# Cutting the minima and maxima of a quantile network so that PSUM copies stand at even distances, and taking the tiles with long lists first

## The chip, the cores and the metric

The kernel runs on one core of a Trainium2 chip. The metric is the device time of one execution in microseconds (us). A core has five engines with a queue of instructions each: TensorE (PE), VectorE (DVE), ScalarE (ACT), GpSimd (POOL) and SyncE (SP). SBUF is the working memory, 128 partitions wide; PSUM is the memory that TensorE writes its products to.

## What is computed

Two graph layers run one after the other over 4096 nodes with 128 features. Layer 0 is a graph attention layer with 8 heads. Layer 1, which the change is about, takes for each node the quartiles of its neighbours' features, feature by feature:

```python
remove = mask & ((rank + 1) % skip[:, None] == 0)
keep = mask & ~remove
n_keep = keep.sum(axis=1)
vals = jnp.where(keep[:, :, None], x[None, :, :], big)
svals = jnp.sort(vals, axis=1)
for q in (0.25, 0.5, 0.75):
    idx = jnp.maximum(jnp.ceil(q * n_keep).astype(jnp.int32) - 1, 0)
    picked = jnp.take_along_axis(svals, idx[:, None, None], axis=1)[:, 0, :]
    agg = agg + w_q * picked
agg = 0.5 * agg + 0.5 * x
out = agg @ W.T + b + x
```

About 32 of 4096 entries in a row of the adjacency matrix are set, so a node has some 32 neighbours.

## The kernel before

The first half of the execution searches the adjacency matrix for each node's neighbours and computes layer 0; the change does not touch it. The nodes are then ordered by their number of neighbours and split into 32 tiles of 128 nodes, one node to a partition, tile 0 with the shortest lists and tile 31 with the longest. `HT[t]` is half the length of the longest list of tile t after the removal; `2 * HT` slots are sorted, from 22 in tile 0 to 62 in tile 31.

A **unit** is what is sorted together: tiles 0 and 1 alone, tiles 2 to 23 in pairs, tiles 24 to 31 alone (`UNITS`, 21 of them). For each unit:

- `fetch_unit` has GpSimd issue one indirect DMA per slot and tile (`vals`, 128 rows of 128 features each, by `gather`, line 178), then one per tile for the nodes' own rows (`xs`). `vals` has two buffers, so the fetch of a unit can start once the unit two before it has read its values.
- `quantile_out` has VectorE run a selection network over the slots: in each of its rounds, minima and maxima of slots at a distance d (line 1117). `groups` joins neighbouring slots, so one instruction covers `c` runs of `m` slots, each slot 128 elements wide in a single tile and 256 in a pair. The first rounds read `vals`, the later ones two work tiles by turns, the last write the slots that can hold a quantile (`goal`).
- After every stretch of minima and maxima that a count (`ran`) puts above `BREATH` = 2.0 us, VectorE copies one element from PSUM (`still`) to `junk` (line 1126).
- ScalarE scales an identity matrix by the weight of each slot (`dg`, line 1136), TensorE sums the slots with it and applies the layer's matrix, ScalarE copies the result to `o`, and `write_out` has GpSimd scatter it to the output (line 187), one DMA per tile.

In GpSimd's queue the fetch of the next unit stands ahead of the scatters of the unit before the current one. The order of instructions on VectorE, TensorE, ScalarE and GpSimd is the order in which the program issues them. `order` sets the sequence of the units: [0], [2,3], [6,7], [10,11], [14,15], [18,19], [22,23], [25], [27], [29], [31], [30], [28], [26], [24], [20,21], [16,17], [12,13], [8,9], [4,5], [1].

Of the kernel before, what the change touches and what calls it, by code (L numbers as in the profile page):

```python
# [63 lines left out]
UNITS = [[0], [1]] + [[t, t + 1] for t in range(2, 24, 2)] + [[t] for t in range(24, NT)]  # L64
# [3 lines left out]
        HT[_t] = max((CAP[t] - 1) // 2 for t in _u)  # L68
LMAX = 2 * max(HT)
SLOTS = max(2 * HT[u[0]] * len(u) for u in UNITS)  # L70
BREATH = 2.0


R_NUM, R_OWN, R_F1 = L, L + 1, L + 2
# [22 lines left out]
def selection_network(n, targets):  # L97


    t = (n - 1).bit_length()  # L100
    stages = []
    p = 1 << (t - 1)
    while p:
        q, r, d = 1 << (t - 1), 0, p
        while True:
            stages.append((d, [i for i in range(n - d) if i & p == r]))
            if q == p:
                break
            d, q, r = q - p, q >> 1, p
        p >>= 1  # L110
    live = set(targets)
    plan = []
    for d, lows in reversed(stages):
        mins = [i for i in lows if i in live]
        maxs = [i for i in lows if i + d in live]
        plan.append((d, mins, maxs))
        for i in mins + maxs:
            live |= {i, i + d}
    return plan[::-1]


def groups(slots):

    runs = []
    for s in slots:
        if runs and s == runs[-1][0] + runs[-1][1]:
            runs[-1][1] += 1
        else:
            runs.append([s, 1])
    out = []  # L130
    i = 0
    while i < len(runs):
        b, n = runs[i]
        j = i + 1
        stride = n
        if j < len(runs) and runs[j][1] == n:
            stride = runs[j][0] - b
            while j < len(runs) and runs[j] == [b + stride * (j - i), n]:
                j += 1
        out.append((b, j - i, stride, n))  # L140
        i = j
    return out


def slots_of(tile_, g, size):

    b, k, stride, n = g
    flat = tile_[:, b * size : (b + (k - 1) * stride + n) * size]
    if k == 1:
        return flat  # L150

    return bass.AP(
        tensor=flat.tensor,
        offset=flat.offset,
        ap=[list(flat.ap[0]), [stride * size, k], [1, n * size]],
    )
# [12 lines left out]
def targets_of(unit):  # L169

    return sorted(set().union(*(quantile_slots(t) for t in unit)))
# [30 lines left out]
def kernel(  # L202
# [15 lines left out]
    nc = tc.nc  # L218
# [65 lines left out]
    parts = adjp.tile([64, N], BF16, name="parts", bufs=1)  # L284
# [155 lines left out]
    kp.release()  # L440


    order = [[t] for t in (0,)] + UNITS[2::2] + UNITS[3::2][::-1] + [UNITS[1]]
    with tc.tile_pool(name="sort", bufs=2) as sp, tc.tile_pool(name="fin", bufs=3) as fp, tc.tile_pool(
        name="fin_ps", bufs=2, space=PSUM
    ) as pp, tc.manual_schedule(engines=ORDERED):
# [2 lines left out]
        still = pp.tile([P, 1], F32, name="still", bufs=1)  # L449
        nc.vector.memset(still, 0.0)  # L450
        late = dict(ident=ident, halfid=halfid, ones=ones, WlT=WlT, bl_b=vecs[:, 3, :], still=still)
# [19 lines left out]
        for nxt in order[1:] + [None]:  # L471
            now = fetched
            if nxt:
                fetched = fetch_unit(nxt)
            if done:
                write_out(*done)
            done = quantile_out(tc, sp, fp, pp, *now, wt, late)
# [602 lines left out]
def quantile_out(tc, sp, fp, pp, unit, vals, xs, wt, late):  # L1080

    nc = tc.nc
    k = len(unit)
    n, size = 2 * HT[unit[0]], k * D
    targets = targets_of(unit)


    where = [vals] * n
    pair = [sp.tile([P, SLOTS * D], F32, name=f"work{i}", bufs=1) for i in range(2)]
    goal = sp.tile([P, TMAX * D], F32, name="goal")  # L1090
    junk = sp.tile([P, 1], F32, name="junk", bufs=1)

    def turn(v):
        return pair[1] if v is pair[0] else pair[0]

    network = selection_network(n, targets)
    final = {}
    for r, (d, mins, maxs) in enumerate(network):
        for i in mins + [i + d for i in maxs]:
            final[i] = r  # L1100
    ran = 0.0
    for r, (d, mins, maxs) in enumerate(network):
        after = list(where)
        for low, slots, op in ((0, mins, ALU.min), (d, maxs, ALU.max)):
            kinds = {}
            for i in slots:
                at = i + low in targets and final[i + low] == r
                kinds.setdefault((id(where[i]), id(where[i + d]), at), []).append(i)
            for (_, _, at), same in kinds.items():
                a, b = where[same[0]], where[same[0] + d]  # L1110
                dst = goal if at else turn(b if low else a)
                parts = groups(same)
                if at:
                    parts = [(i + q * s, 1, m, m) for i, c, s, m in parts for q in range(c)]
                for i, c, s, m in parts:
                    j = targets.index(i + low) if at else i + low
                    nc.vector.tensor_tensor(  # L1117
                        slots_of(dst, (j, c, s, m), size),
                        slots_of(a, (i, c, s, m), size),
                        slots_of(b, (i + d, c, s, m), size),  # L1120
                        op,
                    )
                    ran += 0.06 + c * m * size * 0.00104
                    if ran > BREATH:

                        nc.vector.tensor_copy(junk, late["still"])
                        ran = 0.0
                for i in same:
                    after[i + low] = dst
        where = after  # L1130

    st_ps = pp.tile([P, 2, P], F32, name="st_ps")
    for u, t in enumerate(unit):
        for j, place in enumerate(targets):
            dg = fp.tile([P, P], F32, name="dg", bufs=6)
            nc.scalar.activation(dg, late["ident"], AF.Copy, scale=wt[:, t, place : place + 1])  # L1136
            nc.tensor.matmul(  # L1137
                st_ps[:, u, :],
                lhsT=goal[:, (j * k + u) * D : (j * k + u + 1) * D],
                rhs=dg,  # L1140
                start=(j == 0),
                stop=False,
            )
        nc.tensor.matmul(
            st_ps[:, u, :], lhsT=xs[:, u, :], rhs=late["halfid"], start=False, stop=True
        )
    sT = fp.tile([P, 2, P], F32, name="sT")
    nc.scalar.copy(sT[:, 0:k, :], st_ps[:, 0:k, :])
    o_ps = pp.tile([P, 2, D], F32, name="fo_ps")
    for u in range(k):  # L1150
        nc.tensor.matmul(o_ps[:, u, :], lhsT=sT[:, u, :], rhs=late["WlT"], start=True, stop=False)
        nc.tensor.matmul(
            o_ps[:, u, :], lhsT=late["ident"], rhs=xs[:, u, :], start=False, stop=False
        )
        nc.tensor.matmul(
            o_ps[:, u, :],
            lhsT=late["ones"][0:1, :],
            rhs=late["bl_b"][0:1, :],
            start=False,
            stop=True,  # L1160
        )
    o = fp.tile([P, 2, D], F32, name="o")
    nc.scalar.copy(o[:, 0:k, :], o_ps[:, 0:k, :])  # L1163
    return unit, o
# [226 lines left out]
```

## Time and profile before

| | us |
|---|---|
| median of 3 runs | 3857.79 (3854.88 to 3884.28) |
| the profiled execution | 3857.37 |
| its span | 3855.5 |
| first gather of the quantile stage starts | 1930.2 |
| first minimum of the stage starts | 1959.35 |
| last copy from PSUM in the stage starts | 3845.3 |
| `L178 vals` gathers, 1024: mean / shortest / longest | 1.382 / 0.941 / 4.759 |
| `L1126` copies, 627: shortest / median / longest | 0.139 / 0.148 / 0.154 |
| `L187` scatters to the output, 32: mean | 2.123 |

The profile is of one execution. Its page gives the busy share of each engine in 40 equal slices of the span (one digit each, in tenths, 9 is 90% or more). Tables by stretch give the busy time and, in brackets, the number of instructions of PE matmuls, PE weight loads (PEld), DVE, ACT and POOL, then TensorE's clock, the share of the DMA engines and GB/s. In the order in time a line has the start, the duration, the engine, the source line, the operation with its output and input, and the shape; in square brackets stands how long the engine was idle before and what ended that. "A <- B: us, times" in a list of waits is the time that an engine spent waiting for B.

### The profile page before, as it was taken

What the parts mean: (1) busy time and instruction counts of PE and PEld (TensorE: products, weight loads), DVE (VectorE), ACT (ScalarE), POOL (GpSimd) and SP (SyncE); (2) the same over time, 40 slices, a digit from 0 to 9 for tenths busy, and PEclk for the clock granted to TensorE, in tenths of its full rate; (3) what the DMA queues carried; (4) which work ended last, traced back from release to release, by engine and by line L of the source; (5) the groups of instructions that cost most, each with busy time, mean ns of one, the idle gap of its engine ahead of it and who ended that gap; (6) DMA issues with size and microseconds to landing.
All of it is one profiled execution on the core that took longest, in us unless ns stands there. A gap on an engine that the chain in (4) does not pass through costs nothing. (4 is left out here: it accounts for less than half of the span.)

```text
span 3855.5 us, 21960 instructions
## 1 busy us (share of the span) xinstructions
PE 1253.7 (33%) x5433; PEld 961.2 (25%) x5433; DVE 2671.4 (69%) x6439; ACT 403.4 (10%) x603; POOL 2807.9 (73%) x2388
## 2 busy tenths in 40 slices
PE   6483867863746444455600000000000000000001
PEld 2143534543635444444500000000000000000000
DVE  8774688782522222257436888669999999998788
ACT  3111223210111101111100000000000000000000
POOL 1657674577777777777478888877788887888882
PEclk9975666655665555555555555555555555555555
DMA  6423444322222222222111111111111111111110
GB/s 213 153 88 106 150 139 132 122 54 65 54 55 53 54 53 54 64 58 55 34 47 38 41 39 34 38 42 41 41 38 28 32 35 44 38 35 38 38 40 16
DMA packets 110281, 241.25 MB, mean 63 GB/s; under 512 B 46976, under 2 KB 63360, under 8 KB 101952
## 3 DMA queue, kind: packets, MB, share of 16 engines
q0 software_dynamic: 76160, 160.24, 15.3%
q10 hardware_dynamic: 9360, 67.18, 5.1%
q1 hardware_dynamic: 24624, 12.34, 1.3%
q8 instruction: 45, 0.74, 0.1%
q14 instruction: 92, 0.75, 0.1%
HBM read 228.44 MB, written 11.15 MB: 62 GB/s over the span
## 5 line engine op out<-in xcount | busy, mean ns | idle before, releaser
L178 POOL DMA_INDIRECT vals<-x_d,idx x1024 | 1415.6, 1382 | 314.4 <-issue 303.8
L178 POOL DMA_INDIRECT G<-xt_d,idx x1180 | 1173.6, 995 | 483.4 <-issue 339.9
L1117 DVE TENSOR_TENSOR work<-work 128x256 f32<-128x256 f32 (+7 forms) x1168 | 921.5, 823 | 0.7
L1137 PE MATMUL st_ps<-dg,goal 128*128 128x128 f32 x286 | 71.9, 429 | 1791.9 <-DVE goal L1117 1704.4
L1117 DVE TENSOR_TENSOR work<-work,work 128x512 f32<-128x512 f32 (+4 forms) x820 | 584.3, 738 | 1.3
L1137 PEld LDWEIGHTS st_ps<-dg,goal 128*128 128x128 f32 x286 | 63.7, 324 | 1798.4 <-issue 1797.5
L926 PE MATMUL y<-wide,G 128*128 128x32 f32 (+3 forms) x2360 | 480.1, 382 | 21.9 <-DVE wide L914 21.9
L926 PEld LDWEIGHTS y<-wide,G 128*128 128x128 f32 x2360 | 460.0, 297 | 45.8 <-DVE wide L914 24.2
L869 DVE TENSOR_TENSOR z<-G,f1x 128x128 f32<-128x128 f32 (+2 forms) x92 | 29.9, 335 | 471.6 <-DMA G<-xt_d,idx 468.5
L1117 DVE TENSOR_TENSOR work<-vals 128x768 f32<-128x768 f32 (+11 forms) x64 | 128.8, 2028 | 267.8 <-DMA vals<-x_d,idx 265.7
L574 DVE MAX8 first<-key 128x8 f32<-128x128 f32 x1024 | 227.5, 282 | 112.5 <-PE key L610 112.5
L607 PE MATMUL key<-sgn,markb 128*128 128x512 bf16 x256 | 142.0, 555 | 160.9 <-DVE first L574 107.5
L883 PE MATMUL small<-z,own 128*4 128x32 f32 (+3 forms) x436 | 50.4, 284 | 368.1 <-ACT z L876 368.1
L1136 ACT ACTIVATE dg<-ident,wt 128x128 f32<-128x128 f32 x143 | 47.5, 394 | 1105.0 <-PE st_ps L1137 1104.6
L568 ACT ACTIVATE sgn<-adj_t 128x2048 bf16<-128x2048 int32 x64 | 122.1, 1907 | 343.0 <-PE key L607 328.2
L898 PE MATMUL rz<-rden,ownT 4*128 4x32 f32 (+3 forms) x436 | 107.1, 419 | 117.9 <-DVE rden L894 96.5
L610 PE MATMUL key<-parts,oneb 64*128 64x512 bf16 x256 | 140.6, 550 | 6.3 <-POOL parts L196 6.3
L956 PE MATMUL small<-W_sb,late 128*128 128x128 f32 x512 | 118.9, 426 | 33.6 <-DVE late L953 33.6
L898 PEld LDWEIGHTS rz<-rden,ownT 4*128 4x128 f32 x436 | 94.5, 310 | 134.0 <-DVE rden L894 68.3
L187 POOL DMA_INDIRECT out_dram<-o,own_i x32 | 67.9, 2123 | 79.9 <-ACT o L1163 56.2
L883 PEld LDWEIGHTS small<-z,own 128*4 128x4 f32 x436 | 27.1, 102 | 385.8 <-ACT z L876 373.3
L956 PEld LDWEIGHTS small<-W_sb,late 128*128 128x128 f32 x512 | 110.2, 327 | 44.9 <-DVE late L953 43.9
(179 smaller groups left out, 1879.3 us busy)
## 6 DMA issues: line engine op xcount, KB each, us to landing
adj_t<-in_adj_dram ACTq DMA_DIRECT2D x64, 1024.0 KB
G<-xt_d,idx POOLq DMA_INDIRECT x1180
vals<-x_d,idx POOLq DMA_INDIRECT x1024
R<-rec_d SPq DMA_DIRECT2D x128, 26.2 KB
xt_d<-rec SPq DMA_DIRECT2D x4, 544.0 KB
rec<-in_x_dram SPq DMA_DIRECT2D x4, 512.0 KB
W_sb<-in_L_gnn_W_dram SPq DMA_DIRECT2D x2, 512.0 KB
a_b<-in_L_gnn_a_dram SPq DMA_DIRECT2D x2, 512.0 KB
```

The lines of the kernel that those rows point to most:

```text
L178: nc.gpsimd.indirect_dma_start(out=dst, out_offset=None, in_=rows, in_offset=bass.IndirectOffsetOnAxis(ap=idx, axis=0),)
L187: return nc.gpsimd.indirect_dma_start(out=rows, out_offset=bass.IndirectOffsetOnAxis(ap=idx, axis=0), in_=src, in_offset=None,)
L568: nc.scalar.activation(sgn, adj_t, AF.Sign, accum_out=cnt[:, i : i + 1])
L574: nc.vector.max(first[:, ts(c0 // CW + c, 8)], key[:, ts(c, CW)])
L607: nc.tensor.matmul(key, lhsT=markb, rhs=sgn[:, ts(b, 512)], start=True, stop=False)
L610: nc.tensor.matmul(key, lhsT=oneb[0:64, :], rhs=parts[:, ts(r, 512)], start=False, stop=True)
L883: nc.tensor.matmul(den[0:4, :].rearrange("p (g r h) -> p r g h", r=k // 4, h=H)[:, r], lhsT=own[w][:, ts(r, 4)], rhs=z[:, layer[i] : layer ...
L898: nc.tensor.matmul(rz[:, layer[i] * H : (layer[i] + w) * H], lhsT=ownT[w][:, r, :], rhs=rden.rearrange("p (g r h) -> p r g h", r=k // 4, h ...
L926: nc.tensor.matmul(yf[:, ts(g, c)], lhsT=G[:, col + g - g0, 0:D], rhs=pf[:, ts(g, c)], start=(i == 0 and g % (w // 2) == w // 2 - 1), stop ...
L956: nc.tensor.matmul(o, lhsT=hv[:, h, :], rhs=consts["W1_sb"][:, h, :], start=(h == 0), stop=(h == H - 1))
L1117: nc.vector.tensor_tensor(slots_of(dst, (j, c, s, m), size), slots_of(a, (i, c, s, m), size), slots_of(b, (i + d, c, s, m), size), op,)
L1137: nc.tensor.matmul(st_ps[:, u, :], lhsT=goal[:, (j * k + u) * D : (j * k + u + 1) * D], rhs=dg, start=(j == 0), stop=False,)
```

## The change

The function `then` keeps a count of what VectorE has run since the last copy: 0.148 us for a first minimum or maximum, 0.071 for each further one, and 0.001042 us for each element. An instruction that would take the count over 1.7 us is cut (`cut`) to as many slots as fit in 1.45 us; if not one slot fits, a copy is issued ahead of it. A copy is issued as soon as the count is over 1.25 us.

The order of the units becomes [0], then the single tiles from [24] to [31], then the pairs from [22,23] down to [2,3], and [1].

```diff
--- before.py
+++ after.py
@@ -68,7 +68,12 @@
         HT[_t] = max((CAP[t] - 1) // 2 for t in _u)
 LMAX = 2 * max(HT)
 SLOTS = max(2 * HT[u[0]] * len(u) for u in UNITS)
-BREATH = 2.0
+TT_FIX, TT_EACH, TT_OVER = 0.148, 0.001042, 0.077
+TURN_MIN, TURN_AIM, TURN_MAX = 1.25, 1.45, 1.7
 R_NUM, R_OWN, R_F1 = L, L + 1, L + 2
@@ -140,6 +145,17 @@
         out.append((b, j - i, stride, n))
         i = j
     return out
+def cut(g, room):
+    i, c, s, m = g
+    if c == 1:
+        return [(i, 1, room, room), (i + room, 1, m - room, m - room)]
+    if m > room:
+        return [(i, 1, m, m), (i + s, c - 1, s, m)]
+    q = min(c - 1, room // m)
+    return [(i, q, s, m), (i + q * s, c - q, s, m)]
 def slots_of(tile_, g, size):
@@ -440,7 +456,9 @@
     kp.release()
-    order = [[t] for t in (0,)] + UNITS[2::2] + UNITS[3::2][::-1] + [UNITS[1]]
+    pairs = [u for u in UNITS if len(u) == 2]
+    order = UNITS[:1] + UNITS[2 + len(pairs) :] + pairs[::-1] + UNITS[1:2]
     with tc.tile_pool(name="sort", bufs=2) as sp, tc.tile_pool(name="fin", bufs=3) as fp, tc.tile_pool(
         name="fin_ps", bufs=2, space=PSUM
     ) as pp, tc.manual_schedule(engines=ORDERED):
@@ -1099,6 +1117,14 @@
         for i in mins + [i + d for i in maxs]:
             final[i] = r
     ran = 0.0
+    def then(slots):
+        return ran + TT_FIX + slots * size * TT_EACH - (TT_OVER if ran else 0.0)
+    def turn_of_gpsimd():
+        nc.vector.tensor_copy(junk, late["still"])
     for r, (d, mins, maxs) in enumerate(network):
         after = list(where)
         for low, slots, op in ((0, mins, ALU.min), (d, maxs, ALU.max)):
@@ -1112,7 +1138,19 @@
                 parts = groups(same)
                 if at:
                     parts = [(i + q * s, 1, m, m) for i, c, s, m in parts for q in range(c)]
-                for i, c, s, m in parts:
+                parts = list(parts)
+                while parts:
+                    i, c, s, m = parts.pop(0)
+                    if then(c * m) > TURN_MAX:
+                        room = int((TURN_AIM - then(0)) / (size * TT_EACH))
+                        if ran and room < 1:
+                            turn_of_gpsimd()
+                            ran = 0.0
+                            parts.insert(0, (i, c, s, m))
+                            continue
+                        if c * m > max(1, room):
+                            parts[:0] = cut((i, c, s, m), max(1, room))
+                            continue
                     j = targets.index(i + low) if at else i + low
                     nc.vector.tensor_tensor(
                         slots_of(dst, (j, c, s, m), size),
@@ -1120,10 +1158,9 @@
                         slots_of(b, (i + d, c, s, m), size),
                         op,
                     )
-                    ran += 0.06 + c * m * size * 0.00104
-                    if ran > BREATH:
-
-                        nc.vector.tensor_copy(junk, late["still"])
+                    ran = then(c * m)
+                    if ran > TURN_MIN:
+                        turn_of_gpsimd()
                         ran = 0.0
                 for i in same:
                     after[i + low] = dst
```

## The prediction

> **What bounds the kernel now.** I read the 40 slices first. From slice 21 on (1930 us, where the quantile stage begins) only VectorE (DVE) and GpSimd (POOL) have work:
>
> ```profile
> DVE   8774688782522222257436888669999999998788
> ...
> POOL 1657674577777777777478888877788887888882
> ```
>
> Neither is full throughout: DVE sits at 6 to 8 at both ends of the stage and at 9 in the middle. The table by stretch, cut at the first `work<-vals` of a unit, tells why (columns: length, then busy time and instructions of PE, PEld, DVE, ACT, POOL):
>
> ```profile
> 2327.90:2449.00 121.10, 5.93 (x28) 5.11 (x28) 87.02 (x125) 2.50 (x8) 99.13 (x69) 0.51 0.13 37
> ...
> 2888.30:3029.20 140.90, 6.04 (x23) 4.93 (x22) 140.87 (x291) 3.07 (x10) 121.81 (x63) 0.50 0.11 30
> ...
> 3423.00:3533.10 110.10, 12.12 (x56) 10.23 (x55) 92.42 (x118) 5.81 (x18) 90.94 (x63) 0.53 0.13 37
> ...
> sum 1886.35, PE 121.98 PEld 104.75 DVE 1648.58 ACT 56.59 POOL 1496.70; mean PE 8.13 PEld 6.98 DVE 109.91 ACT 3.77 POOL 99.78
> ```
>
> In a unit of two node tiles (first and third line) DVE works 87 to 92 us and then waits; in [31] (second) it never waits. Over the stage DVE works 1648.6 of 1886.3 us, and the **237.8 us** it is idle are nearly all one wait, seen from the tile it waits for:
>
> ```profile
> DVE work L1117: 233.5, 9
> POOL vals L178: 7.6, 25
> ```
>
> Nine times a sort waits for its gathers. GpSimd does not wait for buffers (7.6 us); it is slow. How slow, the order in time shows. With DVE idle a gather is issued every 1.25 us; with DVE at work:
>
> ```profile
> 2309.05 0.95 POOL L178 DMA_INDIRECT vals<-x_d,idx  x1 [0.30 <-issue]
> 2310.30 0.94 POOL L178 DMA_INDIRECT vals<-x_d,idx  x1 [0.30 <-issue]
> ```
> ```profile
> 2816.92 0.15 DVE L1126 COPY junk<-still 128x1 f32<-128x1 f32 x1
> ...
> 2816.98 0.95 POOL L178 DMA_INDIRECT vals<-x_d,idx  x1 [0.30 <-issue]
> 2816.99 1.25 DVE L1117 TENSOR_TENSOR work<-work,vals 128x1024 f32<-128x1024 f32 x1
> ...
> 2818.16 1.21 DVE L1117 TENSOR_TENSOR work<-vals 128x1024 f32<-128x1024 f32 x1
> 2818.24 1.96 POOL L178 DMA_INDIRECT vals<-x_d,idx  x1 [0.31 <-issue]
> ...
> 2819.30 0.14 DVE L1126 COPY junk<-still 128x1 f32<-128x1 f32 x1
> 2819.37 1.21 DVE L1117 TENSOR_TENSOR work<-work,vals 128x1024 f32<-128x1024 f32 x1
> ```
>
> A gather needs 0.95 us, some 0.05 before its read and 0.90 after it. The one that starts 0.06 after a copy is not held up; the minimum/maximum beside it takes 1.25 instead of 1.21. The one that starts 0.08 after a minimum that follows another is held until the next copy (2819.30 + 0.90 = 2820.20, its end). So **a gather mostly moves on only where a PSUM copy stands**. Copies stand 2.60 us apart on average (1629 us of DVE work by the prices below, 627 copies), up to 4.5 where one instruction has 4096 elements. There are 1024 + 32 gathers and 32 scatters; some 215 fit in DVE's idle time (267 us with the first fetch, / 1.25), the other 870 share about 1590 us: **1.8 us each**, 2.2 in [31] (63 in 140.9 us).
>
> **The skill.** The Trainium skill, "SBUF — State Buffer", section "Who interferes with whom", says that a DVE instruction with two SBUF inputs contends with a GpSimd instruction that reads SBUF, and that whoever comes first holds the shared port for its whole instruction. The trace agrees on the wait (1.96 for 0.95), not on the whole: a gather slips into the first 0.06 us of a minimum, for 0.04 us of it. "VectorE: DVE Perf Modes", section "Why PSUM operands drop a tier", gives PSUM one DVE read port of its own; that a copy from PSUM leaves the shared one free is what the gathers at 2816.98 and 2819.30 show. The same page's section "The TRN2 errata — SBUF-src ops pay a fixed extra latency per instruction" puts a fixed cost on each instruction, so that small ones pay more; in the trace the part that cannot overlap is 0.067 us (1024 elements: 2818.16 to 2819.30 is 1.14 = 1024/960 + 0.07).
>
> **The change, part by part.** Prices, start to start: minimum or maximum 0.067 + elements/960 us; copy 0.07 (2819.30 to 2819.37). Counts are from the built order of instructions.
>
> *Cuts and copies.* Elements stay 1,382,784 a partition = 1440.4 us. Minima and maxima go from 2191 to 2649: 458 x 0.067 = +30.7. Copies from 627 to 1295: 668 x 0.067 = +44.8. Together **+75.4** on DVE: from 1629.2 to 1704.6. That nothing hides: where DVE bounds, it is all paid.
>
> *What DVE adds to the prices.* 1648.6 - 1629.2 is 19 us: near 10 from some 130 waits on the instruction just before, or one before a copy (0.11 or 0.04 each), and near 10 from gathers reading beside a minimum (0.04 each). After, 89 such waits: -4. More gathers fall just behind a copy: if half of 1040 do, 21 us; **+10**, bounds -5 and +35 (every one).
>
> *Distance of copies.* By the prices it becomes 1.32 on average: 450 at 1.20, 361 at 1.27, 185 at 1.33, 284 from 1.40 to 1.67, 14 up to 2.5. A gather comes back 1.25 after its read, so one per copy is a pace of about 1.3. Does that feed DVE? In the pairs ([22,23] to [1]) DVE takes 1024 us. From the fetch of [20,21], which may start once [31] has read its buffer, 652 gathers and scatters have 1120 us: **1.7 us each** is allowed. At 1.3 GpSimd waits for buffers a fourth of the time. So the nine waits go, and what is late next is DVE itself.
>
> *The order.* After [0] comes [24], not [2,3]: 36 gathers before DVE can go on instead of 48. They start at 1959.3, at 1.25 to 1.35 end near 2006, land 1.6 later (as the first fetch did); DVE ends [0] at 1995. Idle **14** (10 to 18), where it was 34.4. Single tiles work DVE 66 to 146 us for 47 to 80 us of gathers at 1.25, so they run DVE-bound from there. [31] right before the pairs gives their gathers a start of over 100 us. Each unit moves whole: its gathers and scatters on POOL's queue, its `dg` scalings on ACT, its matmuls on PE, which are busy 57 and 122 us of 1886 and hide. SP has nothing here. The last unit stays [1], so the tail of 10 us stays. GpSimd's writes of a finished unit stand behind one fetch, as before.
>
> *Waits added.* Nearly every copy now waits for the copy before it (both write `junk`). Behind it stand the next minimum and the gather that needs its turn. That copy has then ended a microsecond before: I take 0, bounds 0 and +0.114 each.
>
> Sum: -237.8 + 14 + 75.4 - 4 + 10 = **-142**. The profiled execution took 3857.4 us (span 3855.5), the median is 3857.8: the same. 3857.4 - 142 = **3715**.
>
> **Rivals.**
> 1. *The turns miss.* At 1.20 a copy comes 0.05 before the gather is back. If that gather is refused it waits a whole turn, 2.4 us a gather. Over the pairs a mean of 2.1 would need 652 x 2.1 = 1369 us, 249 more than the 1120: 3715 + 249 = 3964, slower. It decides from 1.94 (652 x 0.22 = 142); slower by 1% from 2.0. For it: 450 of 1294 distances are 1.20. Against: 2816.98 above asks 0.11 after its copy and passes, and what it costs the minimum (0.04) carries the turn to 1.25. Chance 0.04.
> 2. *DVE pays more.* Every gather costs it 0.045 (+35 on mine) and 10 to 30 us of waiting for gathers stay at the end of the pairs: 3750 to 3780. For it: all 1040 gathers now fall into DVE's work. Chance 0.18.
> 3. *The added wait stalls.* At 0.11 a copy, 1295 copies take 142 us and the gain is gone: 3857, no change. Against: a wait on an instruction a microsecond old costs nothing in the trace. Chance 0.03.
> 4. *The long instructions stay whole*, so gathers still wait 4 us. The built order excludes it: the largest falls from 4096 to 1408 elements.
>
> My forecast (3690 to 3745) has 0.72, still better 0.03. A measurement of this kernel tells about 1% (39 us) from no change. Faster by more 0.92, within 0.04, slower 0.04. The range of 8 in 10 runs from 3690 (no added contention, idle 10, fewer waits) to 3765, into rival 2.
>
> **What would show it.** DVE idle between 1959 and the end near 15 us instead of 238, all before [24]; about 1295 copies and 2649 minima and maxima, DVE busy near 1725; gathers' mean well under 1.38, and "POOL vals <- DVE work" grown to hundreds of us, since buffers then hold GpSimd back. Wrong: gathers of 2 us and more in the pairs (rival 1), minima of 1024 elements lasting 1.25 throughout (2), or copies that start late (3).

## The result, and the profile after

| | before | after |
|---|---|---|
| median of 4 runs, us | 3856.36 (3854.88 to 3884.28) | 3706.74 (3702.95 to 3711.3) |
| the profiled execution, us | 3857.37 | 3702.95 |
| its span, us | 3855.5 | 3701.2 |
| quantile stage: first minimum to last, us | 1959.35 to 3845.7: 1886.35 | 1951.8 to 3691.1: 1739.3 |
| of it VectorE busy / idle, us | 1648.6 / 237.8 | 1723.8 / 15.5 |
| mean of a `vals` gather, us | 1.382 | 1.027 |

The ratio is 0.9599 (0.9575 to 0.9624), estimated from the single executions; the medians are 150 us apart (their quotient is 0.961), where 142 were forecast. Of the 154 us between the two profiled executions, 147.0 lie in the stage. Another 7.6 come from a stage that began earlier, after code that is the same in both: in the eight programs of the table of experiments below the first minimum starts anywhere from 1952.3 to 1966.2, and at 1955.9 in e9, which is the changed kernel again. So it is not counted as an effect of the change.

The 40 slices of the page after, DVE and POOL:

```profile
DVE  8774688782541222127637999999999999999998
POOL 1657674467777777777747777677657565667630
```

From slice 23 on VectorE is full to the end, and POOL has fallen from about 8 to 6 or 7. The table by stretch of the kernel after shows the fetch of [24] behind [0], then [31], then a unit of two tiles, then the whole stage:

```profile
1951.80:2000.90 49.10, 6.95 (x32) 6.21 (x32) 35.23 (x111) 4.11 (x12) 37.82 (x38) 0.53 0.17 50
2507.20:2653.50 146.30, 6.45 (x25) 5.40 (x25) 146.27 (x375) 3.08 (x10) 106.58 (x96) 0.50 0.15 43
2884.80:2983.20 98.40, 6.95 (x33) 5.86 (x32) 98.40 (x193) 3.39 (x11) 64.59 (x64) 0.52 0.15 43
1951.80:3691.10 1739.30, 121.65 (x528) 104.26 (x529) 1723.82 (x3944) 56.59 (x177) 1109.02 (x1064) 0.52 0.14 40
```

The only idle time is in the first line: 35.2 us busy of 49.1. In the pair VectorE works 98.4 of 98.4 us; a pair before took 110 to 121 us for 87 to 92 us of work. In [31] GpSimd now gets 96 instructions through beside a busy VectorE, where it got 63. The tile `vals` of the kernel after, who waited for it, in us and times:

```profile
DVE work L1155: 13.8, 1
POOL vals L194: 12.3, 35
```

Nine waits of 233.5 us have become one of 13.8, ahead of [24]. From the list of GpSimd's own waits after (us, times, longest):

```profile
POOL out_dram L203 <- ACT o L1200: 277.8, 14, 59.1
...
POOL vals L194 <- DVE junk L1126: 23.7, 7, 5.5
...
POOL vals L194 <- DVE work L1155: 2.9, 4, 1.3
```

GpSimd is ahead of VectorE now, but what it waits for is a finished unit, not a free buffer: the scatters of the unit before the current one stand between two fetches in its queue, and once they are out the buffer is nearly free too (26.6 us in 11 waits). This costs nothing, since VectorE has its values. Three groups of the page after (busy us, mean ns, idle time before):

```profile
L194 POOL DMA_INDIRECT vals<-x_d,idx x1024 | 1052.1, 1027 | 337.6 <-issue 298.5
...
L203 POOL DMA_INDIRECT out_dram<-o,own_i x32 | 45.6, 1425 | 297.4 <-ACT o L1200 277.8
...
L1126 DVE COPY junk<-still 128x1 f32<-128x1 f32 x1295 | 194.7, 150 | 0.0
```

With 1.027 us and 0.30 to the next issue a gather comes round every 1.33 us, the mean distance of the copies. In the order in time a pair looks like this:

```profile
3019.88 0.14 DVE L1126 COPY junk<-still 128x1 f32<-128x1 f32 x1
3019.95 1.26 DVE L1155 TENSOR_TENSOR work<-work,work 128x1024 f32<-128x1024 f32 x1
3019.95 0.95 POOL L194 DMA_INDIRECT vals<-x_d,idx  x1 [0.30 <-issue]
3021.13 0.15 DVE L1126 COPY junk<-still 128x1 f32<-128x1 f32 x1
3021.20 1.26 DVE L1155 TENSOR_TENSOR work<-work,work 128x1024 f32<-128x1024 f32 x1
3021.20 0.94 POOL L194 DMA_INDIRECT vals<-x_d,idx  x1 [0.30 <-issue]
3022.38 0.14 DVE L1126 COPY junk<-still 128x1 f32<-128x1 f32 x1
```

A turn is the stretch from one copy to the next. By the prediction's prices this one is 1.20 us long, and GpSimd needs 1.25. Yet copies stand 1.25 apart (3019.88, 3021.13, 3022.38): each gather starts with the minimum behind a copy, makes it 1.26 long instead of 1.21, and so finds the next copy in place. The two have locked.

### The profile page after: what moved, and what is told of

It reads as the page before. It is cut to its first block, busy times and chain, and to the rows that moved or that the text cites. A ratio compares the mean times of both kernels' runs of the same rounds, so it can differ in the third digit from the quotient of the medians.

```text
span 3701.2 us, 23191 instructions
## 1 busy us (share of the span) xinstructions
PE 1228.3 (33%) x5433; PEld 936.3 (25%) x5433; DVE 2746.5 (74%) x7565; ACT 403.4 (11%) x603; POOL 2421.0 (65%) x2388
## 3 DMA queue, kind: packets, MB, share of 16 engines
q0 software_dynamic: 76160, 160.24, 15.5%
## 5 line engine op out<-in xcount | busy, mean ns | idle before, releaser
L194 POOL DMA_INDIRECT vals<-x_d,idx x1024 | 1052.1, 1027 | 337.6 <-issue 298.5
L1155 DVE TENSOR_TENSOR work<-work 128x512 f32<-128x512 f32 (+6 forms) x1405 | 961.0, 714 | 0.4
L1155 DVE TENSOR_TENSOR work<-work,work 128x512 f32<-128x512 f32 (+5 forms) x958 | 606.4, 658 | 0.7
L944 PE MATMUL y<-wide,G 128*128 128x32 f32 (+3 forms) x2360 | 460.3, 371 | 23.9 <-DVE wide L932 23.9
L944 PEld LDWEIGHTS y<-wide,G 128*128 128x128 f32 x2360 | 440.2, 286 | 47.5 <-DVE wide L932 26.3
L203 POOL DMA_INDIRECT out_dram<-o,own_i x32 | 45.6, 1425 | 297.4 <-ACT o L1200 277.8
L1126 DVE COPY junk<-still 128x1 f32<-128x1 f32 x1295 | 194.7, 150 | 0.0
L1155 DVE TENSOR_TENSOR work<-vals 128x1024 f32<-128x1024 f32 (+8 forms) x140 | 138.8, 1009 | 46.4 <-DMA vals<-x_d,idx 46.1
```

Source lines behind the costliest of these rows:

```text
L194: nc.gpsimd.indirect_dma_start(out=dst, out_offset=None, in_=rows, in_offset=bass.IndirectOffsetOnAxis(ap=idx, axis=0),)
L944: nc.tensor.matmul(yf[:, ts(g, c)], lhsT=G[:, col + g - g0, 0:D], rhs=pf[:, ts(g, c)], start=(i == 0 and g % (w // 2) == w // 2 - 1), stop ...
L1155: nc.vector.tensor_tensor(slots_of(dst, (j, c, s, m), size), slots_of(a, (i, c, s, m), size), slots_of(b, (i + d, c, s, m), size), op,)
```

## The experiments

"The kernel before" was run again beside each set on the same chip. Idle time is VectorE's in the stage.

| run | before on that chip | median, us | ratio | minima, copies | VectorE busy / idle, us | mean gather, us |
|---|---|---|---|---|---|---|
| e1_order_only | 3861.77 | 3844.84 | 0.9959 (0.9943 to 0.9975) | 2191, 627 | 1648.2 / 222.6 | 1.391 |
| e2_turns_only | 3861.77 | 3726.80 | 0.9646 (0.9630 to 0.9662) | 2649, 1295 | 1727.5 / 36.1 | 1.013 |
| e3_copies_only | 3861.77 | 3686.23 | 0.9548 (0.9532 to 0.9564) | 2191, 1058 | 1674.7 / 45.3 | 1.243 |
| e4_cuts_only | 3861.77 | 3738.54 | 0.9697 (0.9664 to 0.9729) | 2649, 686 | 1685.6 / 87.5 | 1.304 |
| e9_changed_again | 3862.53 | 3706.04 | 0.9591 (0.9574 to 0.9608) | 2649, 1295 | 1723.9 / 15.4 | 1.030 |
| e10_copy_from_sbuf | 3862.53 | 3716.24 | 0.9615 (0.9597 to 0.9632) | 2649, 1295 | 1732.2 / 15.3 | 1.044 |
| e11_short_turns | 3862.53 | 3934.40 | 1.0182 (1.0152 to 1.0213) | 3563, 1794 | 1809.3 / 152.2 | 1.491 |
| e12_long_turns | 3862.53 | 3673.32 | 0.9495 (0.9468 to 0.9522) | 2250, 1116 | 1681.7 / 17.2 | 1.181 |

**e1_order_only: the new order without the new turns.**

```diff
-    order = [[t] for t in (0,)] + UNITS[2::2] + UNITS[3::2][::-1] + [UNITS[1]]
+    pairs = [u for u in UNITS if len(u) == 2]
+    order = UNITS[:1] + UNITS[2 + len(pairs) :] + pairs[::-1] + UNITS[1:2]
```
(in the kernel before)

> The kernel before with the new order of units alone; minima, maxima and the 627 copies stay as they were. Theory 'turns' (a gather moves on where a copy stands, the order only shortens the first wait): the gathers keep their 1.8 us, the sorts still wait 230 to 280 us in all, time 3830 to 3880 us, about as before. Theory 'order' (the long single lists give the pairs a start that hides their gathers): the waits shrink to 15 to 60 us, 3660 to 3720 us.

The list of waits of this run, its sorts' wait for gathers (32.4 of it ahead of the first unit):

```profile
DVE work L1118 <- DMA vals<-x_d,idx: 245.9, 13, 32.4
```

The waits stay, at 13 places instead of 10: the order moves them and does not remove them. It is worth 17 us alone.

**e2_turns_only: the new turns in the old order.** In the kernel after:

```diff
-    pairs = [u for u in UNITS if len(u) == 2]
-    order = UNITS[:1] + UNITS[2 + len(pairs) :] + pairs[::-1] + UNITS[1:2]
+    order = [[t] for t in (0,)] + UNITS[2::2] + UNITS[3::2][::-1] + [UNITS[1]]
```

> The changed kernel with the order of units of before; cuts and copies stay. Theory 'turns': the gathers take 1.3 us each, only the waits ahead of [2,3] (29 us) and [6,7] (7 us) stay instead of 14 us ahead of [24], so 3707 + 22 = 3729 us (3720 to 3740). Theory 'order': the waits of the first pairs stay as they were, 3800 us or more.

Its table by stretch, the whole stage:

```profile
1955.50:3719.10 1763.60, 117.55 (x528) 100.93 (x529) 1727.54 (x3944) 56.61 (x177) 1088.31 (x1064) 0.52 0.15 40
```

36.1 us idle against 15.5 is the 21 us by which it stands behind the full change: [2,3] with its 48 gathers comes after [0], as before. So the turns carry 135 us and the order 21 on top of them.

**e3_copies_only: a copy as soon as the count is over 1.2 us, nothing cut.** In the kernel after, with its order (there the count is 1.25):

```diff
-TURN_MIN, TURN_AIM, TURN_MAX = 1.25, 1.45, 1.7
+TURN_MIN, TURN_AIM, TURN_MAX = 1.2, 9.0, 99.0
```

> The changed kernel, its order too, without any cut: an instruction keeps its up to 4096 elements, and a copy follows as soon as the count is over 1.2 us (1058 copies, 2191 minima and maxima). Theory 'copies' (the number of copies counts, the cuts little): VectorE has 1658 instead of 1705 us of work, some 45 to 60 us of waiting come up in the last six pairs, 3690 to 3710 us. Theory 'cuts' (the long instructions hold the gathers): the gathers that stand behind the 1.5 to 4.4 us instructions keep the sorts waiting for over 130 us, 3780 us or more.

```profile
1953.50:3673.50 1720.00, 119.10 (x528) 102.12 (x529) 1674.72 (x3249) 56.60 (x177) 1341.50 (x1064) 0.52 0.15 41
```

That line is the whole stage. It is faster than the full change, by 20 us, and a little faster than expected. VectorE works 49 us less than in the kernel after (458 cuts and 237 copies fewer, at 0.067 each: 46.6); its idle time grows by 30, of which 21 are two waits at late pairs: gathers still wait behind instructions of up to 4096 elements, and one gather took 4.89 us. The cuts, then, cost more than they return once copies stand where they can.

**e4_cuts_only: the same cuts, copies as sparse as before.** In the kernel after, the count for the cuts stays, and a second one decides on copies:

```diff
-                    if ran > TURN_MIN:
+                    run += 0.06 + c * m * size * 0.00104
+                    if run > 2.0:
                         turn_of_gpsimd()
+                        run = 0.0
+                    if ran > TURN_MIN:
                         ran = 0.0
```
(and no copy where `room < 1`)

> The changed kernel, its order and its cuts (2649 minima and maxima), but copies by the old rule, one after each 2.0 us (686). Theory 'copies': the gathers must wait for one copy in 2.4 us or slip in between two minima; the sorts wait 80 to 135 us, 3725 to 3780 us. Theory 'cuts' (any start of a short instruction lets a gather in): waits of 15 to 30 us, VectorE 1664 us of work, 3660 to 3680 us.

The order in time in a pair of this run:

```profile
3023.33 0.14 DVE L1126 COPY junk<-still 128x1 f32<-128x1 f32 x1
3023.39 2.40 DVE L1154 TENSOR_TENSOR work<-work,work 128x1024 f32<-128x1024 f32 x2
3023.40 0.94 POOL L194 DMA_INDIRECT vals<-x_d,idx  x1 [0.30 <-issue]
3024.64 1.97 POOL L194 DMA_INDIRECT vals<-x_d,idx  x1 [0.30 <-issue]
3025.72 0.15 DVE L1126 COPY junk<-still 128x1 f32<-128x1 f32 x1
3025.78 2.39 DVE L1154 TENSOR_TENSOR work<-work,work 128x1024 f32<-128x1024 f32 x2
3026.91 0.94 POOL L194 DMA_INDIRECT vals<-x_d,idx  x1 [0.30 <-issue]
```

Two minima stand in one turn here. The gather that asks at 3024.64, 0.12 us into the second one, lasts until 3026.61: the copy at 3025.72 plus 0.90. The one at 3026.91 comes just where the first minimum of the next turn ends and the second begins (3025.78 plus 1.13), and it is not held. So a border between two minima can let a gather in, but not reliably. Call a gather held if it lasts over 1.05 us, and let it have gone on 0.90 us before its end. Of the 457 held gathers of this run, 303 went on at a copy and 145 at such a border. Every copy that a held gather met let it go on; of the borders, 145 did and 319 did not. In the kernel before, 347 of 505 held gathers went on at a copy and 140 at a border, where 217 other borders kept them waiting. What decides at a border is not known.

This run is 106 us better than e1. The likely reason, which no run separates, is shorter turns: no minimum or maximum lasts longer than 1.62 us here, where uncut ones lasted up to 4.43, and 13% of the turns are over 2.6 us, where it was 28% in e1. A cut then has value where it shortens the longest turns.

**e5 to e8** put the source of the copy, its wait and the length of the turns to the test, on a chip on which the kernel before took 4461.13 us instead of 3860. There the first minimum started some 610 us later, after code that is the same in all, and in the stage VectorE waited 33 to 205 times a run for something that the profile names only "remote" or "issue", where on the other chips it does so twice at most. Waits of e6 there:

```profile
DVE work L1159 <- remote: 145.5, 42, 8.2
...
DVE work L1159 <- issue: 126.2, 107, 8.8
```

What slowed that chip is not known, and it did not burden all versions alike: e5 is 3.4% slower there than the kernel before, while the same program is 3.9% faster on another chip (e10). Its stage took 2022.1 us there and 1747.5 in e10. The stage of the kernel before took about 1880 us there, as elsewhere (1886.35). This is an estimate: its 4461.13 us, less the 2570 after which these four programs began the stage and 10 us of tail. So the gain of the change is shown on the other chips alone, and these four times don't answer the questions that they were to answer:

e5_copy_from_sbuf, the edit of e10 below: 4601.78 us, ratio 1.0338 (1.0269 to 1.0407).

> The changed kernel with each of the 1295 copies reading two elements of a tile in SBUF instead of one in PSUM; all else stays. Theory 'PSUM' (the copy serves because it leaves the second SBUF port alone, and a copy from SBUF to SBUF does not): gathers pass at some starts of minima only, mean well over 1.4 us, the sorts wait again, 3800 us or more. Theory 'short instruction' (any instruction of 0.15 us between two minima serves): 3707 us, within 0.5%.

e6_no_junk_wait: 4644.34 us, ratio 1.0399 (1.0344 to 1.0455).

```diff
-    junk = sp.tile([P, 1], F32, name="junk", bufs=1)
+    junk = sp.tile([P, 32], F32, name="junk", bufs=1)
...
-        nc.vector.tensor_copy(junk, late["still"])
+        at = turns[0] % 32
+        turns[0] += 1
+        nc.vector.tensor_copy(junk[:, at : at + 1], late["still"])
```

> The changed kernel with the copies writing 32 different columns by turns, so that nearly none waits for the copy before it (7 waits at copies instead of 1201). If the added wait is free, as I took it: 3707 us, within 0.3%. If it stalls VectorE by up to 0.11 us each: 3570 to 3690 us.

e7_short_turns, the edit of e11: 4620.91 us, ratio 1.0287 (1.0197 to 1.0376).

> The changed kernel with turns of 0.9 to 1.2 us (3563 minima and maxima, 1794 copies), so that most copies stand 0.94 to 1.2 us apart, clearly sooner than a gather comes back (1.25). VectorE's work goes from 1705 to 1799 us by the prices. Theory 'a refused gather takes the next copy, and the pairs have room': gathers of 1.5 to 1.9 us, waits of 15 to 40 us, 3790 to 3820 us. Theory 'misses' (rival 1): with two copies to a gather at 2.0 us and more, waits of over 100 us, 3880 us or more.

e8_long_turns, the edit of e12: 4384.15 us, ratio 0.9829 (0.9780 to 0.9877).

> The changed kernel with a copy as soon as the count is over 1.2 us, but a cut only where an instruction would take it over 2.4 us, to 1.8 (2250 minima and maxima, 1116 copies). By the prices VectorE has 1666 us of work instead of 1705, and by one gather a turn the pairs' gathers still fit: 3660 to 3670 us. If turns of 1.4 to 2.3 us make the gathers late: 3690 to 3740 us.

e5, e7 and e8 were run again as e10 to e12. e6 was not; the kernel after answers its question otherwise (see rival 3 in the next section).

**e9_changed_again: the kernel after, beside e10 to e12.**

> The changed kernel itself, beside the three below on one chip, because the chip of the last four runs was slower altogether (the kernel before took 4461 us there). On a chip like the first: 3700 to 3712 us; on one like the last I expect 4590 to 4640 us, near the two runs there that have its instructions.

3706.04 us, the time of the first measurement.

**e10_copy_from_sbuf: the copy reads SBUF instead of PSUM.**

```diff
-    junk = sp.tile([P, 1], F32, name="junk", bufs=1)
+    junk = sp.tile([P, 2], F32, name="junk", bufs=1)
...
-        nc.vector.tensor_copy(junk, late["still"])
+        nc.vector.tensor_copy(junk, late["ident"][:, 0:2])
```

> The run with copies from SBUF again. Its trace on the slower chip has gathers passing at these copies as at those from PSUM (mean 1.07 us). Theory 'short instruction': within 0.5% of the changed kernel beside it. Theory 'PSUM': slower by 2% or more.

The copies' group on the page of this run, then its order in time:

```profile
L1126 DVE COPY junk<-ident 128x2 f32<-128x2 f32 x1295 | 221.0, 171 | 0.0
```
```profile
3020.74 0.94 POOL L194 DMA_INDIRECT vals<-x_d,idx  x1 [0.30 <-issue]
3020.75 0.20 DVE L1126 COPY junk<-ident 128x2 f32<-128x2 f32 x1
3020.86 1.21 DVE L1155 TENSOR_TENSOR work<-work 128x1024 f32<-128x1024 f32 x1
3021.99 0.94 POOL L194 DMA_INDIRECT vals<-x_d,idx  x1 [0.30 <-issue]
```

Gathers pass just as well. The copy takes 0.20 us beside a gather's read instead of 0.15, and the minimum behind it keeps its 1.21: the same 0.05 is paid at another place. 10 us more in all (8 of them on VectorE). So it need not be PSUM that opens the way: a short instruction with one input between two with two inputs does. Shortness alone is not enough: in e4 a held gather met the border ahead of a minimum or maximum of 128 elements (0.28 us, two inputs) 50 times and went on 9 times. A long instruction with one input was not tried.

**e11_short_turns: turns shorter than a gather.**

```diff
-TURN_MIN, TURN_AIM, TURN_MAX = 1.25, 1.45, 1.7
+TURN_MIN, TURN_AIM, TURN_MAX = 0.9, 1.15, 1.2
```

> The run with turns of 0.9 to 1.2 us again. On the slower chip a gather that came back after 1.25 us had missed the copy at 0.94 and took the one at 1.87 in most cases. By the prices 95 us more of VectorE's work, and 15 to 40 us of waits: 3800 to 3840 us beside 3707. If a missed copy costs more than one turn: over 3880 us.

```profile
3323.98 0.15 DVE L1126 COPY junk<-still 128x1 f32<-128x1 f32 x1
3324.05 0.95 DVE L1155 TENSOR_TENSOR work<-work 128x768 f32<-128x768 f32 x1
3324.18 1.63 POOL L194 DMA_INDIRECT vals<-x_d,idx  x1 [0.30 <-issue]
3324.91 0.15 DVE L1126 COPY junk<-still 128x1 f32<-128x1 f32 x1
3324.98 1.02 DVE L1155 TENSOR_TENSOR work<-work 128x256 f32<-128x256 f32 x2
3325.91 0.15 DVE L1126 COPY junk<-still 128x1 f32<-128x1 f32 x1
...
3326.12 1.64 POOL L194 DMA_INDIRECT vals<-x_d,idx  x1 [0.30 <-issue]
```

More copies than in any other run, and slower than the kernel before. The gather at 3324.18 comes 0.13 into a minimum, waits for the copy at 3324.91 and ends 0.90 after it; when the next one is issued (3326.12) the copy at 3325.91 is past. Every second copy goes unused: in the pairs most gathers stand 1.94 us apart (the median), two turns of 0.94 to 1.0. VectorE's work grows by 85.5 us and its idle time by 137, together the loss of 222 us in the stage. The expectation missed by some 100 us. It had the pace nearly right (the copy at 1.87), but put the waits at 15 to 40 us. The time lies where a missed copy was to cost more than one turn, yet in the lines it costs one. Borders between two minima helped little here: of 759 that a held gather met, 48 let it go on.

**e12_long_turns: turns somewhat longer, cuts only above 2.4 us.**

```diff
-TURN_MIN, TURN_AIM, TURN_MAX = 1.25, 1.45, 1.7
+TURN_MIN, TURN_AIM, TURN_MAX = 1.2, 1.8, 2.4
```

> The run with copies from 1.2 us on and cuts only over 2.4 us again. VectorE has 39 us less to do by the prices than in the changed kernel; with no wait but the one ahead of [24] (15 us): 3655 to 3672 us beside 3707.

Its whole stage, and its order in time:

```profile
1963.70:3662.50 1698.80, 121.27 (x528) 103.96 (x529) 1681.65 (x3366) 56.60 (x177) 1272.78 (x1064) 0.52 0.15 41
```
```profile
3022.49 1.43 POOL L194 DMA_INDIRECT vals<-x_d,idx  x1 [0.30 <-issue]
3023.02 0.15 DVE L1126 COPY junk<-still 128x1 f32<-128x1 f32 x1
3023.09 1.22 DVE L1155 TENSOR_TENSOR work<-work 128x1024 f32<-128x1024 f32 x1
3024.22 0.15 DVE L1126 COPY junk<-still 128x1 f32<-128x1 f32 x1
3024.23 0.94 POOL L194 DMA_INDIRECT vals<-x_d,idx  x1 [0.31 <-issue]
```

The best of all: 399 cuts and 179 copies fewer than in the kernel after (38.7 us by the prices, 42.2 measured), and no idle time comes back, because a gather that waits half a microsecond (1.43 us) is still soon enough. Against the changed kernel on the same chip 3673.32 / 3706.04 = 0.991. It came 1 us above the expected range; its profiled stage began 8 us later than that of e9.

## Why the prediction was right

- **What bounds the kernel** held. Idle time went from 237.8 to 15.5 us, all but 1.7 of it ahead of [24] (forecast 14, measured 13.8). The mechanism is shown by e1 (order alone: idle 222.6), e2 (turns alone: 36.1), e3 (copies without cuts: 45.3) and e4 (cuts without the added copies: 87.5), and by the held gathers, which go on at every copy and only at some borders. The prediction's "mostly" was right, at 347 of 505; its gather at 2818.24, though, asked after a border and so tells nothing of borders.
- **Cuts and copies, +75.4**, and with the two smaller terms +81.4 on VectorE; measured +75.2. The prices held: VectorE's busy time less the sum of prices is 19.4 us before and 19.2 after. What was mis-sized is the +10 for gathers reading beside a minimum. From each instruction's start to the next one's, less its price, over the whole stage: 150 minima and maxima were lengthened before (by over 0.02 us beyond elements/960 + 0.145; 6.7 us together) and 281 after (10.3 us), so +3.6. The prediction took half of 1040. The waits on an instruction just before, or one before a copy, cost 10.8 us before (127) and 7.5 after (88): -3.3, where -4 was taken.
- **Gather pace.** 1.3 us was forecast, and 1.33 measured.
- **Rival 1, the turns miss**, was false here and is true a little further on. At 1.20 the 0.05 us that a gather's read adds to its minimum carries the turn to 1.25, as argued; at 0.94 (e11) that is too little, and every second turn is lost.
- **Rival 2** fell with the 15.5 us of idle time and with those 281 of 2649: minima of 1.25 are not the rule.
- **Rival 3, the added wait**, fell without e6: the copies have 0.0 us of idle time before them, and busy time above the prices did not grow. At 0.11 each, 1295 copies would show 142 us.
- **Rival 4, long instructions left whole**, would have been no loss once copies are added: e3 cuts nothing, e12 little, and both are faster than the full change. The +30.7 for cuts was priced rightly and mostly not needed.
- **One sign was put in the wrong place**: "POOL vals <- DVE work" was to grow to hundreds of us. GpSimd does wait some 280 us, but ahead of its scatters for the sums of a finished unit. The queue's order, which the front part tells (fetch, then the scatters of the unit before), should have given that: whoever waits first in a queue hides the waits behind.
- **Start of the stage, -7.6 us**, was no term of the sum and is not counted as an effect of the change. Sum of the rest: 147.0 against 142.4.
- **The chip** was no term either. On the one of e5 to e8 such a change lost time, and nothing in the prediction foresaw that; that the change was measured on another chip is luck.

One reading of the trace before was too narrow. The copy's source in PSUM was named as what leaves the way free; e10 shows that a two-element copy within SBUF does it too, in a kernel 0.3% slower. In the Trainium skill, "SBUF — State Buffer", section "Who interferes with whom" says that an instruction with at most one SBUF input does not contend with GpSimd outside certain modes, which some copies can enter. The trace of e10 agrees nearly: 0.05 us of contention at such a copy.

## What to carry to other kernels

Where one engine goes on reliably only in gaps that another leaves, look at the period with which it comes back (here 1.25 us) and place the gaps a little closer or further apart than that, never much closer: a gap missed costs a whole turn, so that the run with the most gaps was the slowest. Price the gaps and cuts on the engine that bounds afterwards: once the waits are gone each 0.07 us is paid in full, and the version that cut least while keeping the waits away (e12) was the best. Take placement and splitting apart in the experiment; here the copies alone beat both together.

## What the hardware showed that was not expected

- A gather that starts within 0.02 us of the start of a minimum or maximum behind a copy is not held (214 of 214 in the kernel after). It lengthens that instruction by up to 0.05 us, so that turns of 1.20 become 1.25 by themselves.
- A border between two minima or maxima often keeps a held gather waiting: 217 of 357 times in the kernel before, 319 of 464 in e4, 711 of 759 in e11. A copy next to never does (2 of 742 in e11). Gathers thus lasted up to 4.76 us in the kernel before. In the profile of the kernel after the longest took 2.01, and in e9, the same kernel, a single one took 4.06.
- One chip ran the same versions 15 to 24% slower than the others (4461.13 against 3862.53, 4601.78 against 3716.24), with sorts waiting for "remote" and "issue". There the cuts and copies of the change came out 3 to 4% slower than the kernel before (e5, e6), and only e8, with fewer, 1.7% faster. The cause was not found.
